# Layer 0 of a four-layer gated transformer kernel: value products placed behind the next four heads' scores, the output bias added early, two norms cut into smaller steps

## The chip, the cores and the metric

The kernel runs on one core of a Trainium2 chip. The metric is the time of one execution on the device in microseconds (us), and the number to predict is the median of several executions of the changed kernel. The engines that the text names are PE (TensorE: matrix products and, with an identity matrix, transposes), DVE (VectorE), ACT (ScalarE), POOL (GpSimd) and SP (SyncE, which issues most transfers here). PE writes its results to a small memory, PSUM; DVE or ACT has to copy them out before the PSUM buffer can be used again. Each engine works through its own list of instructions in order. Between engines there are only semaphores: an instruction that waits holds up everything behind it on its engine.

## The reference

The program is a stack of four layers on x of 8 batches x 256 tokens x 512 channels, each layer being `x = x + tanh(g) * attention(layernorm(x))` and then `x = x + tanh(g') * ffn(layernorm(x))`. Only layer 0 is touched by the change. Cut to what matters:

```python
# layer 0, cross attention, 16 heads of 32 channels, quantised linear maps
q = w8a8_linear(layernorm(x), wq, bq)            # per token: s = max|x|/127, round(x/s)
k, v = ctx @ wk.T + bk, ctx @ wv.T + bv
o = softmax(q @ k.T / sqrt(32) + mask) @ v
x = x + tanh(g0) * w8a8_linear(o, wo, bo)        # quantised per token again, then + bo
# layer 0, feed-forward: one of 8 experts of rank 64 per token
lg = layernorm(x) @ Wg.T;  e = argmax(softmax(lg))
x = x + tanh(g1) * 4 * prob[e] * ((layernorm(x) @ A[e].T) @ Bw[e].T)
```

Layers 1 to 3 (linear attention with 64 experts, channel attention with a dense feed-forward, a recurrence with 8 experts) follow and are the same before and after.

## The kernel before

The 2048 tokens lie in 16 tiles `xt[i]` of 128 tokens x 512 channels, which stay in the core's memory. Layer 0 goes through four blocks of 512 tokens (`blk`), each of two batches (`bb` 0 and 1; batch number `b = 2*blk + bb`). `attend0` handles one batch. Its 16 heads are taken in four groups `j` of four. A group is: the scores `s` of its four heads (L521, eight products that use 32 rows of the array each, four side by side), and then for each head `r` two maxima over the scores (L541, DVE), two exponentials with their sums (L546, ACT), four transposes of the probabilities (`pt`, L553, PE), and one copy of them to `pT` (L105 on DVE or L107 on ACT, in turn). After the four heads come the group's value products `oT` (L562), their copy `oTs`, two transposes `o` (L573), and the multiplication by the reciprocal sums into `ao` (L575, L576).

Beside the attention of block `blk` other work is threaded in. After each head, `step()` (L477) advances the projection of the batch before by one step, and a generator `others(blk)` by a rate of steps per head (`due`, L480: 0.65 in block 0, 1.1 in blocks 1 and 2, 0.9 in block 3). `others` mixes (L458) two steps of `tokens()` with one step of `context()`:

- `context()` makes keys (4 steps, L308) and values (4 steps, L313) of the next block, or in the last block keys of layer 1 (`keys1`). One such step is four products of 128x128 by 128x512.
- `tokens()` first waits, with empty steps, until the projection of the batch before is done (`while proj`), then runs the expert layer of block `blk - 1` (`experts`, L344: one step for the norm of four token tiles, two for their transposes `tr_f`, one for the router's logits `lgk`, `lgp`, and twelve for the products `h` and `y` with the experts' weights), and then the queries of block `blk + 1` (`queries`, L321: one step for the norm of four tiles, four in which a tile is quantised and transposed, four for the products `q0ps`).

`project()` (L583) quantises `ao` (two steps), transposes it (`trq_o`, two steps), and multiplies by `wo` (two steps). Each of the last two ends with three operations: DVE scales the product into `y` (L597), POOL adds the bias `gbo` to `y` (L598), POOL adds `y` to `xt[i]` (L599). A norm is: `bn_stats` and `bn_aggr` of each tile on DVE (L160, L163), one addition (`ve`, L167), a power on POOL (`rstd`, L169), and the subtraction and scaling of each tile on DVE (`xn`, L179).

A planner at compile time puts the instructions on the engines' lists. It takes them in the order in which the program makes them, except that an instruction whose inputs and buffers the planner's own clock shows ready can go ahead of one that is not ready. The scores have a raised priority (L517), and the first four of a group may start only when the last maximum of the group before is done (L530). Buffers bound how far this goes: six `pT` tiles, two PSUM banks `tr` (transposes and `oT`), two `ac` (`o` and the threaded work), four `mm` (scores), six tiles `b8` (keys, values, queries, turned tokens), four `xn`.

Of the kernel before, what the change touches and what calls it, by code (L numbers as in the profile page):

```python
# [11 lines left out]
F32 = mybir.dt.float32  # L12
# [3 lines left out]
ALU = mybir.AluOpType  # L16
# [4 lines left out]
P = 128  # L21
C = 512
KC = C // P
B, S = 8, 256
# [25 lines left out]
def flamingo_kernel(ctx: ExitStack, tc: tile.TileContext, a):  # L50
# [210 lines left out]
    def front():  # L261
# [57 lines left out]
                yield  # L319

        def queries(blk, bank):  # L321
            xns = norm(blk, "a0")
            yield
            qxT = qxp.tile([P, KC, BLK], BF16, tag="qx", name=f"qxT{blk}")
            sx_ps = bank(f"sx_ps{blk}")
            for i in range(TB):
                q, s = quantise(xns[i], f"x{blk}_{i}")
                transpose4_q(qxT[:, :, ts(i, P)], q, f"x{blk}_{i}")
                spread(sx_ps[:, ts(i, P)], s, f"x{blk}_{i}")
                yield  # L330
            sx = t2.tile([P, BLK], F32, tag="t2", name=f"sx{blk}")
            nc.scalar.copy(sx, sx_ps)
            Q[blk] = b8.tile([P, KC, BLK], F32, tag="b8", name=f"Q0_{blk}")
            for j in range(KC):
                ps = bank(f"q0ps{blk}_{j}")
                matmul_k(ps, [qT["wq0"][:, k, ts(j, P)] for k in range(KC)], [qxT[:, k, :] for k in range(KC)])
                nc.vector.scalar_tensor_tensor(Q[blk][:, j, :], ps, swq[:, j : j + 1], sx, ALU.mult, ALU.mult)
                nc.gpsimd.tensor_scalar(Q[blk][:, j, :], Q[blk][:, j, :], bq[:, j : j + 1], None, ALU.add)
                yield
# [1 line left out]

        AB = []

        def experts(blk, bank, halves=1):  # L344
            A, Bw = AB
            xnT = b8.tile([P, KC, BLK], F32, tag="b8", name=f"xnT_f0{blk}")
            n = TB // halves
            for half in range(halves):
                xns = norm_of(range(blk * TB + half * n, blk * TB + half * n + n), f"f0{blk}_{half}_")
                yield  # L350
                for i in range(n):
                    transpose4(xnT[:, :, ts(half * n + i, P)], xns[i], f"f0{blk}_{half * n + i}")
                    if i % 2:
                        yield
            lg = logits(xnT, wg, f"f0{blk}")
            yield
            best = best_of_8(lg, 1, f"f0{blk}")

            _, rz = softmax_8(lg, f"f0{blk}")
            nc.vector.tensor_scalar(rz, rz, tg[:, 4:5], 4.0, ALU.mult, ALU.mult)  # L360
            h, hT = {}, {}

            def first(i):
                ps = bank(f"h0_{blk}_{i}")
# [12 lines left out]

            def second(i):
                ps = bank(f"y0_{blk}_{i}")
                matmul_k(ps, [hT[i][:, k, :] for k in range(KC)], [Bw[:, k, :] for k in range(KC)])  # L380
                add_scaled(blk * TB + i, ps, rz[:, i : i + 1])


            first(0)
            yield
            for i in range(TB):
                if i + 1 < TB:
                    first(i + 1)
                    yield
                turned(i)  # L390
                yield
                if i:
                    second(i - 1)
                    yield
            second(TB - 1)
            yield
# [9 lines left out]
        def others(blk):  # L406
# [15 lines left out]

            def tokens():
                if blk:
                    while proj:
                        yield
                    yield from experts(blk - 1, actile)
                if blk + 1 < NB:
                    yield from queries(blk + 1, actile)
                else:  # L430
                    for _ in range(2):
                        yield next(last_experts)

            def context():
                if blk + 1 < NB:
                    yield from keys(blk + 1, actile)
                    yield from values(blk + 1, actile)
                else:
                    yield from keys1(0, actile)
                    yield next(last_keys)  # L440

            yield from mix(tokens(), context(), 2)

# [8 lines left out]
                nc.scalar.activation(K1[:, j, :], ps, AF.Identity, bias=first1["bk"][:, j : j + 1])  # L452
                yield

        last_experts = experts(NB - 1, mmtile, 2)
        last_keys = keys1(1, mmtile)

        def mix(one, two, n):  # L458
# [10 lines left out]
                    yield  # L469

        aos = []
        proj, last_max = [], []
        for blk in range(NB):
            gen = others(blk)
            due = [0.0]
# [1 line left out]
            def step():  # L477
                if proj and next(proj[0], 0) is not None:
                    proj.pop()
                due[0] += (0.65, *(NB - 2) * (1.1,), 0.9)[blk]  # L480
                while due[0] >= 1.0:
                    due[0] -= 1.0
                    next(gen, None)
# [1 line left out]
            if blk == 0:  # L485
                next(gen)
            for bb in range(BLK // S):
                one = attend0(blk, bb, Q[blk], K[blk], V[blk], qT["wo0"], gswo, gbo, aos[0], last_max, step)
                proj.append(one)
            for _ in gen:  # L490
                pass

        for n, _ in enumerate(proj[0]):
            if n == 1:
                next(last_keys)
        next(last_experts)
        for _ in last_keys:
            pass
        for _ in last_experts:
            pass  # L500

    def attend0(blk, bb, Q, K, V, woT, gswo, gbo, aos, last_max, step):

# [7 lines left out]
        s16 = sm.tile([P, 2, NH], F32, tag="s16", name=f"s16_{b}")  # L511
        rs = sm.tile([P, 2, NH], F32, tag="rs16", name=f"rs_{b}")
        ao = aos[:, b % 2]
        for j in range(KC):
            nm = f"{b}_{j}"
            ps = [mm.tile([P, 2, S], F32, tag="mm", name=f"s_{nm}_{r}") for r in range(4)]
# [20 lines left out]
            for r in range(4):  # L537
# [15 lines left out]
                        nc.tensor.transpose(pt_ps[:, lt, nt, :], pr[:, nt, ts(lt, P)], ident)  # L553
                pT.append(ptp.tile([P, 2, S], F32, tag="pT", name=f"pT_{nm}_{r}"))
                evac(pT[r], pt_ps.rearrange("p l n q -> p l (n q)"))
                step()
            last_max.append(one)
            oT_ps = tr.tile([P, S], F32, tag="tr", name=f"oT_{nm}")
            for lt in range(2):
                for r in range(4):  # L560
                    rows = slice(HD * r, HD * r + HD)
                    nc.tensor.matmul(  # L562
                        oT_ps[rows, :],
                        V[:, bb * 2 + lt, ts(4 * j + r, HD)],
                        pT[r][:, lt, :],
                        start=(lt == 0),
                        stop=(lt == 1),
                    )
            oT = sm.tile([P, S], F32, tag="oT", name=f"oTs_{nm}", bufs=2)
            evac(oT, oT_ps)  # L570
            o = ac.tile([P, 2, 4, HD], F32, tag="ac", name=f"o_{nm}")
            for nt in range(2):
                nc.tensor.transpose(o[:, nt].rearrange("p h d -> p (h d)"), oT[:, ts(nt, P)], ident)  # L573
            heads = slice(4 * j, 4 * j + 4)
            nc.vector.reciprocal(rs[:, :, heads], s16[:, :, heads])  # L575
            nc.vector.tensor_tensor(  # L576
                ao[:, :, ts(j, P)].rearrange("p n (h d) -> p n h d", d=HD),
                o,
                rs[:, :, heads].unsqueeze(3).to_broadcast([P, 2, 4, HD]),
                ALU.mult,  # L580
            )

        def project():  # L583
            qs, qoT = [], []
# [7 lines left out]
            for nt in range(2):  # L592
# [2 lines left out]
                i = b * 2 + nt  # L595
                y = t2.tile([P, C], F32, tag="t2", name=f"y_{b}_{nt}")
                nc.vector.scalar_tensor_tensor(y, ps, qs[nt][1], gswo, ALU.mult, ALU.mult)  # L597
                nc.gpsimd.tensor_tensor(out=y, in0=y, in1=gbo, op=ALU.add)  # L598
                nc.gpsimd.tensor_tensor(out=xt[i], in0=xt[i], in1=y, op=ALU.add)  # L599
                yield  # L600

        return project()
# [43 lines left out]

    def logits(xnT, w, name):

        part = ac.tile([P, BLK], F32, tag="ac", name=f"lgk_{name}")
        last = None  # L650
        for k in range(KC):
# [3 lines left out]
            last = one  # L655
        turned = t2.tile([P, BLK], F32, tag="t2", name=f"lgt_{name}")
        evac(turned, part)
        ps = ac.tile([P, TB, 8], F32, tag="ac", name=f"lgp_{name}")
        for i in range(TB):
            nc.tensor.matmul(ps[:, i, :], turned[:, ts(i, P)], pick8, start=True, stop=True)  # L660
        lg = sm.tile([P, TB, 8], F32, tag="lg8", name=f"lg_{name}", bufs=2)
        nc.vector.tensor_copy(lg, ps)
        return lg
# [1780 lines left out]
```

## Time and profile before

| what | before |
|---|---|
| median of 6 runs | 2644.27 us (2637.74 to 2646.49) |
| the profiled execution, its own time | 2644.52 us |
| span from its first to its last instruction | 2642.7 us, mean granted PE clock 0.971 |
| PE, DVE, ACT, POOL busy over the span | 94%, 48%, 24%, 34% |
| layer 0's attention | first scores at 53.6 us, last value products from 508.9 us |
| layer 0's last expert product | issued from 552.4 us, layer 1's first products from 559.3 us |

The page of a profile gives busy time by engine for the whole span and for 40 slices of 66 us each; layer 0 fills the first eight. Another view gives the same for any stretch of time, with the clock that PE was granted there as a share of full speed. A third lists who waited for whom; "PE s L521 <- DVE n L541: 3.4, 2, 1.7" says that PE sat idle before `s` of line 521 for 3.4 us in all, in 2 places, 1.7 us the longest, and that DVE's `n` of line 541 ended the wait. The timeline gives instructions in order of time, each with its start, its duration, engine, line, operation and tiles, and in brackets the idle time of its engine just before it. PE's ends are modelled, so a PE that is busy all the time is not necessarily at its peak.

### The profile page before, as it was taken

To read this page: it belongs to the slowest core of one execution; us is meant where nothing else is said; L and a number is where in the kernel's file an instruction comes from. 1 tells how busy PE (TensorE), PEld (TensorE's weight loads), DVE (VectorE), ACT (ScalarE), POOL (GpSimd) and SP (SyncE) were. 2 spreads that over 40 slices of the span, in tenths; PEclk is the share of its full clock that TensorE was granted. 3 is DMA by queue.
4 is the path that set the end of the run, shared out by engine and by line. 5 is a ranking of instruction groups with operands and counts; after the bars stand their busy time and mean duration, and the time that the engine had idled before them with its cause. 6 is when DMAs were issued, how large, how long until landed. Compare 5 with 4: busy or idle time off the path is not lost. (4 is left out here: it accounts for less than half of the span.)

```text
span 2642.7 us, 29842 instructions
## 1 busy us (share of the span) xinstructions
PE 2475.2 (94%) x10389; PEld 1272.5 (48%) x10404; DVE 1277.9 (48%) x3518; ACT 643.6 (24%) x1451; POOL 901.6 (34%) x843
## 2 busy tenths in 40 slices
PE   7889898899999979999999899899999999999997
PEld 3445454456655535545555344444444444455553
DVE  6656565536656442222222650767677766211111
ACT  1534344311111112222222111222222222111110
POOL 1110211111344344656665110231534252444542
PEclk9999999998999989999999999999999999999999
DMA  5000010112112127999997741112022212788984
GB/s 219 5 21 25 17 41 5 33 37 80 50 33 65 44 80 219 243 263 267 286 256 169 236 168 68 40 72 104 32 96 91 89 37 52 236 292 291 322 280 89
DMA packets 102180, 333.75 MB, mean 126 GB/s; under 512 B 23288, under 2 KB 25721, under 8 KB 93827
## 3 DMA queue, kind: packets, MB, share of 16 engines
q0 software_dynamic: 48256, 148.74, 21.1%
q1 hardware_dynamic: 50354, 178.73, 19.3%
q10 hardware_dynamic: 3408, 4.25, 0.5%
q8 instruction: 87, 1.43, 0.2%
q14 instruction: 75, 0.61, 0.1%
HBM read 283.35 MB, written 66.88 MB: 133 GB/s over the span
## 5 line engine op out<-in xcount | busy, mean ns | idle before, releaser
L1335 PE MATMUL gu<-w,eb 128*128 128x352 f32 (+1 forms) x1064 | 240.7, 463 | 3.4 <-DMA w<-in_w 3.4
L216 PE MATMUL h2p<-xnT_f,p 128*128 128x512 f32 x512 | 226.9, 598 | 5.7 <-issue 4.4
L216 PE MATMUL o2f<-p,h 128*128 128x512 f32 x512 | 226.0, 595 | 3.3 <-ACT h L1628 3.2
L1370 POOL DMA_INDIRECT acc<-eb,who x94 | 147.4, 1568 | 134.5 <-DVE eb L105 107.5
L1012 POOL DMA_INDIRECT table<-pay,rowi x128 | 125.3, 979 | 138.8 <-PE v L216 44.5
L1335 PEld LDWEIGHTS gu<-w,eb 128*128 128x128 f32 (+1 forms) x1064 | 129.8, 159 | 72.3 <-issue 19.5
L546 ACT ACTIVATE pr<-pr,n 128x256 f32<-128x256 f32 x256 | 127.9, 501 | 149.5 <-DVE n L541 144.6
L216 PEld LDWEIGHTS h2p<-xnT_f,p 128*128 128x128 f32 x512 | 97.0, 192 | 123.4 <-issue 118.5
L216 PEld LDWEIGHTS o2f<-p,h 128*128 128x128 f32 x512 | 95.7, 190 | 122.6 <-issue 114.7
L1387 POOL DMA_INDIRECT xg<-xnd,who x94 | 99.4, 1057 | 64.0 <-PE ehp L1355 20.2
L227 DVE SCALAR_TENSOR_TENSOR x<-o2f,tg,x 128x512 f32<-128x512 f32 x64 | 46.9, 741 | 125.2 <-PE o2f L216 123.7
L598 POOL TENSOR_TENSOR y<-y,gbo 128x512 f32<-128x512 f32 x16 | 20.3, 1271 | 245.4 <-DVE y L597 237.9
L1984 PE MATMUL g_r<-w3gu,xgT 128*128 128x352 f32 (+1 forms) x336 | 102.5, 467 | 0.7 <-ACT xgT L107 0.7
L169 POOL TENSOR_TENSOR rstd_a<-ve_a,mhalf 128x4 f32<-128x4 f32 x15 | 15.7, 1043 | 253.9 <-DVE ve_a L167 252.7
L541 DVE CUSTOM_DVE_ANT_0 pr<-s,mask 128x256 f32<-128x256 f32 x256 | 96.8, 417 | 11.1 <-PE s L521 6.7
L1984 PE MATMUL u_r<-w3gu,xgT 128*128 128x352 f32 (+1 forms) x336 | 100.0, 459 | 0.0
L1993 DVE SCALAR_TENSOR_TENSOR h_r<-a_r,share,u_r 128x352 f32<-128x352 f32 x33 | 19.2, 580 | 160.7 <-PE u_r L1984 152.1
L2010 PE MATMUL d_r<-w3d,hT_r 128*128 128x512 f32 (+3 forms) x252 | 96.1, 596 | 0.0
L1628 ACT ACTIVATE h<-h2p,b 128x512 f32<-128x512 f32 x64 | 43.4, 686 | 213.5 <-PE h2p L216 213.3
L553 PE MATMUL pt<-ident,pr 128*128 128x128 f32 x512 | 85.3, 286 | 9.8 <-ACT pr L546 5.8
L1406 PE MATMUL ed<-w,eb 128*128 128x512 f32 (+1 forms) x266 | 91.5, 601 | 1.6 <-DVE eb L1356 1.6
L553 PEld LDWEIGHTS pt<-ident,pr 128*128 128x128 f32 x512 | 59.6, 143 | 64.8 <-issue 28.4
(586 smaller groups left out, 4729.5 us busy)
## 6 DMA issues: line engine op xcount, KB each, us to landing
w<-in_w SPq DMA_DIRECT2D x64, 960.0 KB
p<-in_p SPq DMA_DIRECT2D x64, 512.0 KB
acc<-xnd SPq DMA_DIRECT2D x48, 256.0 KB
more<-acc SPq DMA_DIRECT2D x48, 256.0 KB
xnd<-xn_f SPq DMA_DIRECT2D x32, 256.0 KB
wd<-in_wd SPq DMA_DIRECT2D x64, 96.0 KB
ctxTa<-in_ctxT SPq DMA_DIRECT2D x4, 1024.0 KB
x<-in_x SPq DMA_DIRECT2D x16, 256.0 KB
```

The costliest lines, as they stand in the source:

```text
L216: one = nc.tensor.matmul(ps, lhsT[k], rhs[k], start=(k == 0), stop=(k == n - 1))
L227: return nc.vector.scalar_tensor_tensor(xt[i], ps, scale, xt[i], ALU.mult, ALU.add)
L541: one = nc.vector.tensor_tensor_reduce(pr[:, nt, :], ps[r][:, nt, :], mask[:, nt, :], -1.0, -LOW, ALU.add, ALU.min, n16[:, nt, h : h + 1],)
L546: nc.scalar.activation(pr[:, nt, :], pr[:, nt, :], AF.Exp, bias=n16[:, nt, h : h + 1], scale=-1.0, accum_out=s16[:, nt, h : h + 1],)
L553: nc.tensor.transpose(pt_ps[:, lt, nt, :], pr[:, nt, ts(lt, P)], ident)
L1012: one = nc.gpsimd.indirect_dma_start(out=table[:, :], out_offset=bass.IndirectOffsetOnAxis(ap=rows, axis=0), in_=choice, in_offset=None, b ...
L1335: one = nc.tensor.matmul(gu[part, 0 : 2 * I1], xT[:, k, part], e.gu[:, k, :], start=(k == 0), stop=(k == KC - 1))
L1370: one = nc.gpsimd.indirect_dma_start(out=acc[0][:, :], out_offset=bass.IndirectOffsetOnAxis(ap=index[:stop, col : col + 1], axis=0), in_=s ...
L1387: nc.gpsimd.indirect_dma_start(out=xg, out_offset=None, in_=xnd[:, :], in_offset=bass.IndirectOffsetOnAxis(ap=who[:, col : col + 1], axis= ...
L1406: one = nc.tensor.matmul(ps[n][part, :], t.hT[rows, k, part], wd, start=(k == 0), stop=(k == 1))
L1984: one = nc.tensor.matmul(ps[part, 0:I3], xTt[:, k, part], wgu[k][:, g, :], start=(k == 0), stop=(k == KC - 1))
L2010: one = nc.tensor.matmul(ps[part, :], hT[:cn, n, part], wd[n][:cn], start=(n == 0), stop=(n == 2))
```

## The change

All of it is in layer 0.

1. The part of `attend0` that follows the four heads (value products, copy, transposes, division) becomes a function `outputs(j, pT)`. It is put in a list `late` and called in the first head of the next group, behind that head's `pT` copy and ahead of its `step()`. For the last group of a batch that is the first head of the next batch, or a call after the loop.
2. The bias `gbo` is added to `xt[i]` on POOL at the start of each batch's `attend0`. `project()` loses its bias addition, and its addition to `xt[i]` moves from POOL to DVE in the second batch of a block (`bb` 1).
3. `experts` norms two tiles at a time in every block (the argument `halves` goes), one step for each tile's statistics and one for the two scalings. Only the second two tiles, those of the batch still being projected, wait for `proj`. The logits take two more steps (`logits_steps`). `queries` gets one step per tile for its statistics.
4. The rates per head rise from 1.1 to 1.45 and from 0.9 to 1.1. In the last block `tokens()` takes one step of `last_keys` and four of `last_experts` in place of two; `context()` loses its step of `last_keys`. After the loop three steps of `last_experts` follow the projection in place of one.

```diff
         def queries(blk, bank):
-            xns = norm(blk, "a0")
+            for stats in stats_of(range(blk * TB, blk * TB + TB), f"a0{blk}"):
+                yield
+            xns = normed(stats, f"a0{blk}")
             yield
...
-        def experts(blk, bank, halves=1):
+        def experts(blk, bank):
             A, Bw = AB
             xnT = b8.tile([P, KC, BLK], F32, tag="b8", name=f"xnT_f0{blk}")
-            n = TB // halves
-            for half in range(halves):
-                xns = norm_of(range(blk * TB + half * n, blk * TB + half * n + n), f"f0{blk}_{half}_")
-                yield
-                for i in range(n):
-                    transpose4(xnT[:, :, ts(half * n + i, P)], xns[i], f"f0{blk}_{half * n + i}")
-                    if i % 2:
+            for half in range(2):
+                if half:
+                    while proj:
                         yield
-            lg = logits(xnT, wg, f"f0{blk}")
+                name = f"f0{blk}_{half}_"
+                for stats in stats_of(range(blk * TB + half * 2, blk * TB + half * 2 + 2), name):
+                    yield
+                xns = normed(stats, name)
+                yield
+                for i in range(2):
+                    transpose4(xnT[:, :, ts(half * 2 + i, P)], xns[i], f"f0{blk}_{half * 2 + i}")
+                yield
+            lg = yield from logits_steps(xnT, wg, f"f0{blk}")
             yield
...
             def tokens():
                 if blk:
-                    while proj:
-                        yield
                     yield from experts(blk - 1, actile)
                 if blk + 1 < NB:
                     yield from queries(blk + 1, actile)
                 else:
-                    for _ in range(2):
+                    yield next(last_keys)
+                    for _ in range(4):
                         yield next(last_experts)
...
                     yield from keys1(0, actile)
-                    yield next(last_keys)
...
-                due[0] += (0.65, *(NB - 2) * (1.1,), 0.9)[blk]
+                due[0] += (0.65, *(NB - 2) * (1.45,), 1.1)[blk]
...
+        late.pop()()
         for n, _ in enumerate(proj[0]):
             if n == 1:
                 next(last_keys)
-        next(last_experts)
+        proj.pop()
+        for _ in range(3):
+            next(last_experts)
...
         ao = aos[:, b % 2]
+        for i in range(b * 2, b * 2 + 2):
+            nc.gpsimd.tensor_tensor(out=xt[i], in0=xt[i], in1=gbo, op=ALU.add)
+        def outputs(j, pT):
+            oT_ps = tr.tile([P, S], F32, tag="tr", name=f"oT_{nm}")
...
                 evac(pT[r], pt_ps.rearrange("p l n q -> p l (n q)"))
+                if late:
+                    late.pop()()
                 step()
             last_max.append(one)
-            oT_ps = tr.tile([P, S], F32, tag="tr", name=f"oT_{nm}")
...
+            late.append(lambda j=j, pT=pT: outputs(j, pT))
...
                 nc.vector.scalar_tensor_tensor(y, ps, qs[nt][1], gswo, ALU.mult, ALU.mult)
-                nc.gpsimd.tensor_tensor(out=y, in0=y, in1=gbo, op=ALU.add)
-                nc.gpsimd.tensor_tensor(out=xt[i], in0=xt[i], in1=y, op=ALU.add)
+                (nc.vector if bb else nc.gpsimd).tensor_tensor(out=xt[i], in0=xt[i], in1=y, op=ALU.add)
                 yield
...
+    def logits_steps(xnT, w, name):
...
         evac(turned, part)
+        yield
         ps = ac.tile([P, TB, 8], F32, tag="ac", name=f"lgp_{name}")
         for i in range(TB):
             nc.tensor.matmul(ps[:, i, :], turned[:, ts(i, P)], pick8, start=True, stop=True)
+        yield
         lg = sm.tile([P, TB, 8], F32, tag="lg8", name=f"lg_{name}", bufs=2)
```

More of the change, by code (lines that the diff above doesn't have):

```diff
@@ L453, in keys1 @@
                 yield
-        last_experts = experts(NB - 1, mmtile, 2)
+        last_experts = experts(NB - 1, mmtile)
         last_keys = keys1(1, mmtile)
@@ L471, in front @@
         aos = []
-        proj, last_max = [], []
+        proj, last_max, late = [], [], []
         for blk in range(NB):
@@ L487, in front @@
             for bb in range(BLK // S):
-                one = attend0(blk, bb, Q[blk], K[blk], V[blk], qT["wo0"], gswo, gbo, aos[0], last_max, step)
+                one = attend0(blk, bb, Q[blk], K[blk], V[blk], qT["wo0"], gswo, gbo, aos[0], last_max, late, step)
                 proj.append(one)
@@ L500, in front, with attend0 @@
             pass
-    def attend0(blk, bb, Q, K, V, woT, gswo, gbo, aos, last_max, step):
+    def attend0(blk, bb, Q, K, V, woT, gswo, gbo, aos, last_max, late, step):
         b = blk * (BLK // S) + bb
@@ L513, in attend0 @@
         ao = aos[:, b % 2]
+        for i in range(b * 2, b * 2 + 2):
+            nc.gpsimd.tensor_tensor(out=xt[i], in0=xt[i], in1=gbo, op=ALU.add)
+        def outputs(j, pT):
+            nm = f"{b}_{j}"
+            oT_ps = tr.tile([P, S], F32, tag="tr", name=f"oT_{nm}")
+            for lt in range(2):
+                for r in range(4):
+                    rows = slice(HD * r, HD * r + HD)
+                    nc.tensor.matmul(
+                        oT_ps[rows, :],
+                        V[:, bb * 2 + lt, ts(4 * j + r, HD)],
+                        pT[r][:, lt, :],
+                        start=(lt == 0),
+                        stop=(lt == 1),
+                    )
+            oT = sm.tile([P, S], F32, tag="oT", name=f"oTs_{nm}", bufs=2)
+            evac(oT, oT_ps)
+            o = ac.tile([P, 2, 4, HD], F32, tag="ac", name=f"o_{nm}")
+            for nt in range(2):
+                nc.tensor.transpose(o[:, nt].rearrange("p h d -> p (h d)"), oT[:, ts(nt, P)], ident)
+            heads = slice(4 * j, 4 * j + 4)
+            nc.vector.reciprocal(rs[:, :, heads], s16[:, :, heads])
+            nc.vector.tensor_tensor(
+                ao[:, :, ts(j, P)].rearrange("p n (h d) -> p n h d", d=HD),
+                o,
+                rs[:, :, heads].unsqueeze(3).to_broadcast([P, 2, 4, HD]),
+                ALU.mult,
+            )
         for j in range(KC):
@@ L555, in attend0 @@
                 evac(pT[r], pt_ps.rearrange("p l n q -> p l (n q)"))
+                if late:
+                    late.pop()()
                 step()
             last_max.append(one)
-            oT_ps = tr.tile([P, S], F32, tag="tr", name=f"oT_{nm}")
[L559 to L581, printed above, removed]
+            late.append(lambda j=j, pT=pT: outputs(j, pT))
         def project():
@@ L647, in logits @@
     def logits(xnT, w, name):
+        steps = logits_steps(xnT, w, name)
+        while True:
+            try:
+                next(steps)
+            except StopIteration as end:
+                return end.value
+    def logits_steps(xnT, w, name):
         part = ac.tile([P, BLK], F32, tag="ac", name=f"lgk_{name}")
```

## Prediction

> **What bounds the kernel now.** I read the page first, for the engine that fills the span and for the clock.
>
> ```profile
> PE 2475.2 (94%) x10389; PEld 1272.5 (48%) x10404; DVE 1277.9 (48%) x3518; ACT 643.6 (24%) x1451; POOL 901.6 (34%) x843
> PE   7889898899999979999999899899999999999997
> PEclk9999999998999989999999999999999999999999
> ```
>
> PE is the bound, and layer 0 (slices one to eight) has more 8s in PE's row than the rest. Then layer 0 by stretches; the columns are length, busy time of PE, weight loads, DVE, ACT and POOL (with counts), and PE's granted clock.
>
> ```profile
> 155.00:188.00 33.00, 25.61 (x163) 14.24 (x162) 21.89 (x71) 14.40 (x45) 7.09 (x6) 0.95 0.01 1
> 188.00:267.00 79.00, 76.08 (x424) 40.00 (x424) 51.27 (x174) 33.74 (x106) 6.29 (x5) 1.00 0.06 21
> 279.00:313.00 34.00, 25.32 (x166) 14.15 (x165) 21.06 (x72) 14.56 (x46) 7.08 (x6) 0.95 0.01 1
> 313.00:392.00 79.00, 75.42 (x422) 39.81 (x423) 52.25 (x174) 32.89 (x103) 6.21 (x5) 1.00 0.13 47
> 404.00:429.00 25.00, 17.95 (x120) 9.90 (x120) 14.74 (x52) 12.45 (x43) 6.08 (x5) 0.87 0.00 1
> 520.00:532.00 12.00, 8.39 (x25) 3.50 (x24) 3.61 (x8) 1.78 (x3) 3.82 (x4) 0.72 0.18 74
> ```
>
> The middle of a block (188 to 267, 313 to 392) is full: PE is busy 96% of it. The loss sits near the start of blocks 1, 2 and 3 (7.4, 8.7 and 7.1 us of idle PE) and in the tail (3.6), and there the clock is low too. The waits of PE between 53 and 552 us say on what; of these lines the last number is the longest wait.
>
> ```profile
> PE oT L562 <- DVE pT L105: 7.4, 7, 4.7
> PE tr_f L194 <- DVE xn_f__0_4455 L179: 3.6, 1, 3.6
> PE s L521 <- DVE ve_f__2594 L167: 2.4, 1, 2.4
> PE s L521 <- DVE ve_f__1538 L167: 2.3, 1, 2.3
> ```
>
> Four single gaps, one in each of those stretches, together 4.75 + 3.61 + 2.40 + 2.33 = 13.1 us (starts 425.7, 525.9, 293.5, 169.5). The timeline shows what stands before one of them.
>
> ```profile
> 286.58 1.27 POOL L598 TENSOR_TENSOR y<-y,gbo 128x512 f32<-128x512 f32 x1 [10.50 <-DVE y L597]
> 287.93 1.27 POOL L599 TENSOR_TENSOR x<-x,y 128x512 f32<-128x512 f32 x1
> 289.17 1.27 POOL L598 TENSOR_TENSOR y<-y,gbo 128x512 f32<-128x512 f32 x1
> 289.24 0.69 DVE L160 BATCH_NORM_STATS2 bn_f__2_2588<-x 128x6 f32<-128x512 f32 x1 [0.77 <-POOL x L599]
> 290.51 1.26 POOL L599 TENSOR_TENSOR x<-x,y 128x512 f32<-128x512 f32 x1
> 291.81 0.69 DVE L160 BATCH_NORM_STATS2 bn_f__3_2591<-x 128x6 f32<-128x512 f32 x1 [1.88 <-POOL x L599]
> 293.46 1.15 PE L521 MATMUL s<-K,Q 32*128 32x256 f32 x16 [2.40 <-DVE ve_f__2594 L167]
> ```
>
> POOL's four additions take 5.2 us in a row. DVE's statistics wait for them, and behind these on DVE's list stand the maxima of the running heads (292.50, 292.91), for which ACT and then PE wait.
>
> **The change part by part.** The sum is made against the profiled execution, 2644.52 us (span 2642.7, 1.8 around it), which lies 0.25 above the median.
>
> *Bias and addition.* In the second batch of a block the way from `y` to the statistics is now one DVE addition. Nearest row: `V<-v0ps,bv`, also 128x512, 0.69 us. From the end of the second `y` to the start of the last statistics took 287.78 to 291.81, 163.91 to 167.94, 415.46 to 419.50 (4.0 each) and 518.7 to 523.2 (4.5); with one addition it is 0.7, so 3.3 and 3.8 us go. A gap can close by no more: 2.33 + 2.40 + 3.3 + 2.8 (in the last, 0.83 us of DVE waiting for the power on POOL stays) = 10.8 us. Late next are gaps of the same stretches, 2.71 us at 298.6 (`tr_f` after `pT`) and 1.59 at 174.7, in which four tiles are scaled in a row ahead of the maxima. I take three quarters, **-8.1**; ends 0 and -10.8. The eight additions cost DVE 8 x 0.69 = 5.5 us, hidden where DVE is busy 64% (21.9 of 33); uncovered they cost 5.5, which offsets a part of this term. POOL has 16 bias additions of 1.27 us as before, at the start of a batch; there its list also holds the queries' bias (1.59 each), for which scores wait. At block 2's start the last of these ended at 276.07 and the scores of the next group began at 279.47, so 2 x 1.27 fits; if not, 2.5 us in each of three blocks.
>
> *Clock.* Lost at the low clock in the four stretches: 0.05 x 33 + 0.05 x 34 + 0.13 x 25 + 0.28 x 12 = 10.0 us. I take **-4**: half of what follows the four gaps (8.3; the rest is a drop at 409, elsewhere). Ends 0 and -10. On this the Trainium skill (TensorE: Matmul & The Clock Gate, "HAM oscillation") speaks against me: it has the clock halved by gaps over about 3.4 us, so shortening 2.33 and 2.40 would earn no clock, and this term would be some 1.7 us smaller. The trace has low clock in both stretches, 0.95, with no gap there over 2.71.
>
> *Steps.* I laid the steps of blocks 1 and 2 out in the program's order, a head at a time. PE: a group of heads 4.2 us (16 transposes at 0.108 start to start, `s` 1.07, `oT` 1.00, `o` 0.4), a key, value or expert product 8 x 0.429 = 3.43, four transposes 0.43, a query product 4 x 0.216 = 0.86. DVE: a group 6.2 (eight maxima at 0.417 + 0.084, two copies at 0.69, 0.8 for the rest). Before: 35 steps in 32 heads, four of them empty; two query products are left over and run bare at the end. After: 46 steps, two empty, none left. In the first eight heads PE work goes from 18.3 to 21.7 us, into a stretch that idles 7.4 to 8.7: up to -3.4 in each of two blocks. In the last eight heads now stand only the queries: PE 13.6 against DVE 29.8 us, where before two expert products were among them, 18.8 against 30.5 with 1.7 left over. PE can idle 16.2 there instead of 11.7 (+1.7 bare is in the block either way): up to +4.5 in each. The planner softens both, since it lets ready work go ahead: queries' statistics of block 3 (`bn_a`) ran at 293.3, far ahead of their step. I take **+2.2**, the sum of both ends; ends -6.8 and +9. Block 0 gets four more steps at an unchanged rate (21 in 20.8), one value step is left over, not needed before the second batch: 0. The extra `ve` and power in three blocks, 0.17 and 1.04 us, have a step between them and the scaling: 0; if DVE waits, 1.2 each, as at 421.8.
>
> *Value products.* Their waits for `pT` (7.4 + 1.9) and those of `o` for `oTs` (5.5) can shrink, but the 4.75 is counted above, so 10.1 is left, and the planner already has the scores ahead: those of the group at 250.4 precede the value products of the group before, at 259.1. I take **-2**; ends -5.1 (all of the `oT` part bar 4.75) and, at seven changes of batch, DVE waiting for `o` before quantising, now in the same step: up to 2.3 us each on DVE, of which PE feels what the quarter of maxima behind it is late, +4. Buffers: four `pT` stay until one head into the next group, which has two more; the third head's copy would wait for the value products, put two heads (2 x 3.9 us) earlier: 0, uncovered one wait of 1.07. The values tile is held one head longer, while keys and queries of its block are free already: 0.
>
> *Moves.* `last_keys` and `last_experts` change places by a few steps, with the same products: 0. No moved step issues a transfer, so SP's and ACT's lists keep their order; the mask's load stays first in a batch. Layer 1's `Wv` is issued at 514.2 and used at 559.3, 45 us of cover.
>
> Sum: -8.1 - 4 + 2.2 - 2 = -11.9, so 2632.6 for the profiled execution and 2632 for the median.
>
> **Rivals.**
>
> 1. *Queries alone become the bound* (the other side). Place: last eight heads of blocks 1 and 2. Price +9 if the planner keeps the program's order. For it: DVE 29.8 against PE 13.6. Against: `bn_a` at 293.3. It decides when the other terms give less than 9 us; without them the time is 2653.5.
> 2. *The change hardly changes the order*: scores already run ahead of value products, statistics ahead of their steps. Then only the POOL part counts in the tail, 2.8, and the rest cancels: 2642.
> 3. *The starts of the blocks fill up*: all ends on the good side, -10.8 - 10 - 6.8 - 5.1 = -32.7, 2612. For it: PE fills 96% where it has threaded work. Against: the starts keep maxima, quantising and norms on one DVE.
>
> **How the numbers follow.** Forecast 0.50 (its own range 2622 to 2639), rival 1 0.22, rival 2 0.15, rival 3 0.13 (2612 to 2622). The range runs from 2612 (all gains) to 2655, rival 1 with half of the three extra power waits (1.8); beyond it I leave some 0.17. A change within 0.2% (5.3 us) is about what a measurement cannot tell from none. Faster by more: forecast 0.47, rival 3 0.13, some of rival 2 0.04, together 0.64. Within: the rest of rival 2, 0.11, and bits of the forecast and rival 1, 0.03 and 0.02: 0.16. Slower: 0.20.
>
> **What the profile after would show.** If the first part is right, no `bn_f` in an odd batch waits for POOL, and the gaps of 2 to 5 us before `s`, `oT` and `tr_f` at the block starts are gone, with clock 1.00 there. If the steps are right, scores of a block start closer together early on and PE stays over 90% busy in its last eight heads; if rival 1 is, those heads show PE under 60% and DVE over 90%. The rest of the program, from the first `v<-Wv` to the end, should keep its length of about 2083 us. I am wrong if DVE's list in the new order puts norms or quantising ahead of the maxima elsewhere, or if layers 1 to 3 change length, which no term here holds.

## The result and the profile after

| | before | after |
|---|---|---|
| median | 2644.18 us (43 runs, 2636.86 to 2650.97) | 2653.58 us (20 runs, 2645.82 to 2660.36) |
| ratio to before | | 1.0034, 95% interval 1.0026 to 1.0043 |
| span of the profiled execution | 2642.7 us | 2657.3 us |
| first `s` | 53.6 us | 56.8 us |
| end of the last `oT` of layer 0 | 510.0 us | 535.6 us |
| first `v<-Wv` of layer 1 | 559.3 us | 578.7 us |
| from there to the end | 2083.4 us | 2078.6 us |

The change made the kernel 0.34% slower, some 9 us, where 2632 us and a gain were forecast. The loss lies in layer 0: 3.2 us before the first scores and 22.4 us more until the last value products, of which the tail gives 6.2 back. That leaves 19.4 us, more than the 9 by which the medians differ, since a profile shows one execution: the rest of the program, the same code in both, was 4.8 us shorter in this one, and 5.0 us longer (2088.4 us) in a second profiled execution of the changed kernel. Two rows of the page after:

```profile
PE 2486.4 (94%) x10391; PEld 1273.9 (48%) x10404; DVE 1289.5 (49%) x3529; ACT 644.2 (24%) x1451; POOL 896.2 (34%) x838
...
PEclk8989999999999899999999999999999999999999
```

PE's busy sum is 11.2 us larger with two instructions more, and PEclk has an 8 in slices one and three, where it had 9s. Layer 0 by stretches (length; busy time of PE, weight loads, DVE, ACT, POOL with counts; then PE's clock):

```profile
142.00:192.00 50.00, 42.75 (x235) 21.67 (x236) 29.43 (x95) 19.16 (x60) 3.41 (x3) 0.93 0.06 22
192.00:287.00 95.00, 87.17 (x459) 45.06 (x459) 57.54 (x190) 34.97 (x109) 11.23 (x9) 0.95 0.05 18
287.00:325.00 38.00, 30.98 (x203) 16.84 (x208) 26.03 (x89) 19.03 (x60) 5.46 (x5) 0.96 0.00 1
325.00:414.00 89.00, 81.21 (x450) 42.47 (x446) 59.88 (x189) 33.03 (x104) 11.23 (x10) 1.00 0.12 42
414.00:447.00 33.00, 27.08 (x188) 14.22 (x189) 24.40 (x84) 18.03 (x58) 5.27 (x4) 0.95 0.00 1
447.00:516.00 69.00, 63.19 (x328) 32.57 (x328) 36.52 (x124) 25.46 (x80) 3.26 (x3) 0.92 0.01 5
```

The stretches that began the blocks (142, 287, 414) still idle, by 7.3, 7.0 and 5.9 us. What is new is the middle of blocks 1 and 2: 7.8 us of idle PE in 192 to 287 and 7.8 in 325 to 414, where 2.9 and 3.6 were idle in the 79 us that were shown of each before, and a clock of 0.92 in the last block's threaded part. The waits of PE name it, before (53 to 552 us) and after (53 to 572 us):

```profile
PE pt L553 <- ACT pr L546: 5.8, 12, 1.2
```

```profile
PE pt L590 <- ACT pr L583: 21.4, 19, 2.8
PE pt L590 <- ACT pT L107: 7.0, 4, 3.2
```

`pt` waiting for ACT's exponential was 5.8 us in 12 places before. It is 21.4 us in 19. The four single gaps behind POOL's additions, which the forecast set out to remove (13.1 us), are gone but for 0.9 us in the tail, and none of the statistics `bn_f` of an odd batch waits for POOL any more. PE's idle time in gaps over 0.1 us, from the first scores to the first `Wv` product, is 54.6 us against 53.1: it has moved, not shrunk. The timeline in one of the new gaps (start, duration, engine, line, operation; in brackets the idle time before and what ended it):

```profile
252.28 0.69 DVE L373 TENSOR_TENSOR h0s<-h,best_f 128x512 f32<-128x512 f32 x1 [3.06 <-PE h L216]
252.89 0.41 DVE L578 CUSTOM_DVE_ANT_0 pr<-s,mask 128x256 f32<-128x256 f32 x1
...
253.34 0.51 ACT L583 ACTIVATE pr<-pr,n 128x256 f32<-128x256 f32 x1 [4.19 <-DVE n L578]
...
254.00 0.44 PE L590 MATMUL pt<-ident,pr 128*128 128x128 f32 x2 [1.76 <-ACT pr L583]
...
254.37 0.62 PE L530 MATMUL oT<-pT,V 128*32 128x256 f32 x2
...
255.29 1.06 PE L530 MATMUL oT<-pT,V 128*32 128x256 f32 x14
```

PE ends the expert product `h`. DVE multiplies it, takes the first maxima of the new group, ACT takes the exponential, and until that is there PE has 1.76 us of nothing. The value products of the group before, all of whose inputs are there, come behind the first two transposes of the first head's `pt` on PE's list. The scores of this group had been done since 246.9; it is not for them that PE waits.

The same group (the sixth of block 1) before, from its timeline:

```profile
231.25 1.07 PE L562 MATMUL oT<-pT,V 128*32 128x256 f32 x16
231.35 0.69 DVE L367 TENSOR_TENSOR h0s<-h,best_f 128x512 f32<-128x512 f32 x1 [2.74 <-PE h L216]
231.96 0.41 DVE L541 CUSTOM_DVE_ANT_0 pr<-s,mask 128x256 f32<-128x256 f32 x1
...
232.65 0.51 ACT L546 ACTIVATE pr<-pr,n 128x256 f32<-128x256 f32 x1
...
232.81 0.44 PE L573 MATMUL o<-ident,oTs 128*128 128x128 f32 x2 [0.49 <-ACT oTs L107]
...
233.08 0.38 PE L216 MATMUL wo<-qT,qoT 128*128 128x512 bf16 x1
...
233.51 0.38 PE L553 MATMUL pt<-ident,pr 128*128 128x128 f32 x2
```

DVE waits for `h` and takes the same maximum, ACT the same exponential; but PE has the value products, `o` and a product of `wo` in the meantime, idles 0.49 us before `o`, and `pt` follows without a wait that counts. The value products were the work that covered the chain from `h` to the exponential.

### The profile page after: what moved, and what is told of

The parts are those of the page before. It is cut to its first block, busy times and chain, and to the rows that moved or that the text cites. A ratio compares the mean times of both kernels' runs of the same rounds, so it can differ in the third digit from the quotient of the medians.

```text
span 2657.3 us, 29856 instructions
## 1 busy us (share of the span) xinstructions
PE 2486.4 (94%) x10391; PEld 1273.9 (48%) x10404; DVE 1289.5 (49%) x3529; ACT 644.2 (24%) x1451; POOL 896.2 (34%) x838
## 5 line engine op out<-in xcount | busy, mean ns | idle before, releaser
L590 PE MATMUL pt<-ident,pr 128*128 128x128 f32 x512 | 89.3, 290 | 31.0 <-ACT pr L583 21.4
L614 POOL TENSOR_TENSOR x<-x,y 128x512 f32<-128x512 f32 x8 | 10.2, 1276 | 241.2 <-DVE y L613 241.1
```

## The experiments

Five theories were set against each other. V: the place of the value products, behind the first head's `pt`, is the loss. W: it is their lateness as such, wherever they stand. S: the smaller steps and the higher rates of steps are. B: the early bias additions are. P, added after the first set: POOL's additions beside DVE's scaling delay the starts of the blocks. The sets of runs were made on different chips. In the second, the kernel before takes 2604.37 us (11 runs), so across sets only ratios to it compare.

### First set: each part alone, and the change without its first part (before: 2644.64 us)

`late_only`: before, with the value products deferred and nothing else.

```diff
                 evac(pT[r], pt_ps.rearrange("p l n q -> p l (n q)"))
+                if late:
+                    late.pop()()
                 step()
             last_max.append(one)
-            oT_ps = tr.tile([P, S], F32, tag="tr", name=f"oT_{nm}")
...
+            late.append(lambda j=j, pT=pT: outputs(j, pT))
```

> Before, with part 1 alone: the value products of a group are called behind the next group's first head. Theory V (the value products no longer stand between a group's scores and its first transposes, so PE waits there for the exponentials): slower than before by 5 to 14 us, PE's wait of the transposes pt for the exponentials pr between 53 and 575 us goes from 5.8 us to over 15, and PE's time at half clock in layer 0 from 20 us to over 30. Theory S (the steps and rates are the loss): within 5 us of before. Theory B (the bias additions on POOL are the loss): within 5 us of before.

`no_late`: after, with the value products back at the end of their own group.

```diff
-                if late:
-                    late.pop()()
                 step()
             last_max.append(one)
-            late.append(lambda j=j, pT=pT: outputs(j, pT))
+            outputs(j, pT)
```

> The changed kernel with part 1 undone: value products straight after their four heads, all else as changed. Theory V: at or under the time of before, 2630 to 2644 us, with the wait of pt for pr back under 10 us. Theory S: 2649 to 2660 us, as changed. Theory B: 2649 to 2660 us.

`bias_only`: before, with the bias added at the start of a batch and DVE's addition in odd batches.

```diff
+        for i in range(b * 2, b * 2 + 2):
+            nc.gpsimd.tensor_tensor(out=xt[i], in0=xt[i], in1=gbo, op=ALU.add)
...
-                nc.gpsimd.tensor_tensor(out=y, in0=y, in1=gbo, op=ALU.add)
-                nc.gpsimd.tensor_tensor(out=xt[i], in0=xt[i], in1=y, op=ALU.add)
+                (nc.vector if bb else nc.gpsimd).tensor_tensor(out=xt[i], in0=xt[i], in1=y, op=ALU.add)
```

> Before, with part 2 alone: bias added on POOL at the start of each batch, addition to x on DVE in every second batch. In the changed profile the scaling xn_a beside these additions took 1.01 us on average, up to 1.50, against 0.55 us without them, and layer 0's first products came 2.3 us later. Theory B: slower than before by 5 to 12 us. Theories V and S: from 6 us faster (the four gaps behind POOL gone) to 2 us slower (the late start).

`steps_only`: before, with the two norms cut into steps and the new rates.

```diff
-            xns = norm(blk, "a0")
+            for stats in stats_of(range(blk * TB, blk * TB + TB), f"a0{blk}"):
+                yield
+            xns = normed(stats, f"a0{blk}")
...
-                due[0] += (0.65, *(NB - 2) * (1.1,), 0.9)[blk]
+                due[0] += (0.65, *(NB - 2) * (1.45,), 1.1)[blk]
```

> Before, with parts 3 and 4 alone: norms in smaller steps, logits in three, higher rates, last_experts earlier. Theory S (queries stand alone in the last eight heads of blocks 1 and 2, where PE starves): slower than before by 5 to 12 us, PE under 75% busy in those heads. Theories V and B: from 8 us faster to 3 us slower.

| kernel | median | ratio to before (95%) |
|---|---|---|
| `late_only` | 2671.08 us | 1.0108 (1.0086 to 1.0130) |
| `no_late` | 2632.65 us | 0.9962 (0.9947 to 0.9977) |
| `bias_only` | 2644.73 us | 1.0009 (0.9996 to 1.0023) |
| `steps_only` | 2639.99 us | 0.9985 (0.9972 to 0.9997) |

The deferral alone costs 26.4 us, more than the whole change loses and well over the 5 to 14 us that V expected; without it the change gains 12.0 us. S falls: the steps are worth a small gain. B falls as a cause of the loss: the bias part is worth nothing either way. The waits of PE in `late_only` (first scores to first `Wv` product) carry the verdict:

```profile
PE pt L581 <- ACT pr L574: 24.2, 18, 4.4
```

The parts do not add up: 26.4 + 0.1 - 4.7 is 21.8, and the change loses 9. The larger part of this lies between the bias and the steps, which give 0.1 and -4.7 us alone and -12.0 together (`no_late`). The deferral costs 26.4 us alone and some 21 on top of the two (24 in the third set). Why the two are worth more together than apart, no run here shows.

### Second set: where the value products stand (before: 2604.37 us)

`ahead`: after, with the deferred products moved by a few lines, from behind the first head's transposes to ahead of them.

```diff
+                if late:
+                    late.pop()()
                 pt_ps = tr.tile([P, 2, 2, P], F32, tag="tr", name=f"pt_{nm}_{r}")
...
                 evac(pT[r], pt_ps.rearrange("p l n q -> p l (n q)"))
-                if late:
-                    late.pop()()
                 step()
```

> The changed kernel with one move: the call of the value products in the next group's first head stands ahead of that head's transposes pt and no longer behind them and their copy. Theory V (PE's list has lost the work between the scores and the first transposes): PE's wait of pt for the exponentials pr is back under 10 us, time 2628 to 2644 us, near the kernel without part 1 (2632.65). Theory W (lateness as such: pT tiles held longer, ao and so the projection late): 2649 to 2660 us, as changed (2653.58).

Measured: 2593.16 us, 0.9958 (0.9944 to 0.9972). The loss is gone, as V expected: PE's waits for the exponential before `pt` fall from 21.4 us to 5.4, and waits of `oT` for `pT` come back, 14.9 us. It is no better than having them at the end of their own group (0.9962 in the first set). It does not separate V from W, for the planner lets the value products go almost as early as in `no_late`: from the end of a group's last `pT` copy to its first value product there are 0.46 us on average, against 0.36 in `no_late` and 1.70 in the change. What speaks against W is in the traces of the third set: the projection, which lateness would hold up, makes PE wait 3.9 us before `trq_o` and `wo` in the change and 3.5 without the deferral. That is an argument, not a test.

`fill`: after, with eight needless transposes of the identity ahead of each first head's `pt`.

```diff
+                if r == 0:
+                    for n in range(8):
+                        nc.tensor.transpose(pt_ps[:, n // 4, n // 2 % 2, :], ident, ident)
                 for nt in range(2):
```

> The changed kernel with eight extra transposes of the identity matrix ahead of the transposes of each group's first head, 32 x 8 x 0.109 = 28 us of needless work on PE, which stand where PE waits for the exponentials. Theory C (half of the loss is PE's clock, halved after stretches with such waits): the time lost to the low clock between the first scores and layer 1's first values, 22.2 us in the changed profile, falls under 15 us, and the kernel is slower than the changed one by less than 14 us. Theory I (the clock has nothing to do with these waits): clock loss stays at 19 us or more and the kernel is slower by 14 us or more.

Measured: 2626.16 us, 1.0087 (1.0068 to 1.0106). Against the change's 1.0034 that is 14 us for 28 us of added work, from ratios of two chips. Side by side with the change it is in the third set.

`bias_later`: `no_late`, with the two bias additions of a batch held until the last maximum of the batch's first group.

```diff
-        for i in range(b * 2, b * 2 + 2):
-            nc.gpsimd.tensor_tensor(out=xt[i], in0=xt[i], in1=gbo, op=ALU.add)
...
         for j in range(KC):
+            if j == 1:
+                for i in range(b * 2, b * 2 + 2):
+                    add = nc.gpsimd.tensor_tensor(out=xt[i], in0=xt[i], in1=gbo, op=ALU.add)
+                    tc.add_manual_dep(add.ins, last_max[-1].ins.name, ...)
```

> The changed kernel without part 1 and with the bias additions on POOL held until the last maximum of the batch's first four heads, so that none runs beside the scaling xn_a. Theory P (POOL's additions slow DVE's scaling: 16 scalings from 1.0 us back to 0.55, first scores 2 to 3 us earlier): 2624 to 2631 us, 2 to 8 us under the kernel without part 1 (2632.65). Theory Q (the slower scalings are hidden, apart from the start): 2630 to 2635 us.

Measured: 2589.13 us, 0.9946 (0.9928 to 0.9964).

`ahead_later`: `ahead` with the same edit to the bias additions.

> Both: value products in the next group's first head ahead of its transposes, and the bias additions held back as in the run before. If both theories V and P hold: 2622 to 2632 us, the fastest of all. If the value products so placed are worse than straight after their heads: above that run by 3 us or more.

Measured: 2591.23 us, 0.9953 (0.9935 to 0.9970). Both ratios lie a little below those of their parents (0.9962, 0.9958), within the intervals, so P was left undecided by this set.

### Third set: four kernels side by side (before: 2644.31 us, 18 runs)

> The changed kernel unchanged, so that it stands on one chip with the next three. If the ratio of a kernel to the kernel before belongs to the kernel and not to the chip, it is 1.0034 again (1.0026 to 1.0043). If the chip decides how much the clock gives away, it is lower on a chip whose times are shorter, and less than 22 us go to the half clock in layer 0.

> The changed kernel with eight needless transposes of the identity ahead of each first head's own transposes, 28 us of added TensorE work, once more beside the changed kernel itself. If TensorE idles there for want of work and nothing else, the added work lies in the idle time: within 7 us of the changed kernel. If half of it fits, 14 us above it (the ratio of the first look, 1.0087 against 1.0034). If the stretch is full, 28 us above it.

> The changed kernel with the value products back at the end of their own group. Theory V (the place of the value products is the whole loss): 0.9962 again, 19 us under the changed kernel on the same chip. If that gain was the chip's, it shrinks to under 10 us here.

> The kernel without late value products, with the two bias additions of a batch held until the last maximum of the batch's first group. Theory P (POOL's additions beside DVE's scaling delay the starts of the blocks): 0.9946 again, 3 to 5 us under the kernel without late value products. The rival (the slower scaling is off the path, and holding the additions only moves them): within 2 us of it.

| kernel | median | ratio to before (95%) |
|---|---|---|
| the change again | 2650.52 us | 1.0023 (1.0011 to 1.0035) |
| `fill` again | 2659.12 us | 1.0054 (1.0035 to 1.0072) |
| `no_late` again | 2626.43 us | 0.9932 (0.9913 to 0.9950) |
| `bias_later` again | 2625.25 us | 0.9932 (0.9910 to 0.9954) |

V a third time: 24.1 us between the change and the same without its deferral, where 19 had been expected. The change's own ratio lies below its first, 1.0034, with intervals that overlap. Where the 24.1 us lie is seen in two tables of the same program stretches, cut at the same instructions (the first line is the whole, from the first `s` to the first `Wv` product; then block 1 from its third group to its end, block 2's first two groups, block 2 from its third group, and block 3 from its third group to its last `oT`). The change:

```profile
55.50:573.80 518.30, 461.49 (x2569) 240.91 (x2581) 317.61 (x1057) 210.43 (x653) 51.71 (x61) 0.97 0.08 25
189.50:283.20 93.70, 85.75 (x471) 44.65 (x473) 58.91 (x196) 36.46 (x114) 11.32 (x10) 0.98 0.06 18
283.20:316.90 33.70, 26.87 (x175) 14.57 (x176) 23.22 (x79) 15.88 (x49) 5.34 (x4) 1.00 0.00 1
316.90:410.30 93.40, 85.33 (x471) 44.91 (x473) 61.87 (x199) 36.06 (x115) 11.14 (x10) 0.98 0.12 40
439.60:530.70 91.10, 84.44 (x460) 44.05 (x461) 47.14 (x162) 38.54 (x120) 3.26 (x3) 0.94 0.01 4
```

And `no_late`:

```profile
55.40:545.20 489.80, 447.21 (x2569) 237.21 (x2581) 316.35 (x1057) 209.97 (x653) 51.21 (x60) 0.99 0.08 27
181.50:270.70 89.20, 84.78 (x475) 45.67 (x477) 60.73 (x196) 35.48 (x114) 11.18 (x10) 0.98 0.06 19
270.70:303.30 32.60, 27.03 (x176) 14.36 (x177) 23.13 (x79) 15.78 (x49) 5.29 (x4) 1.00 0.00 1
303.30:390.90 87.60, 83.06 (x471) 44.44 (x473) 59.73 (x199) 37.07 (x115) 11.14 (x10) 1.00 0.12 43
421.20:502.10 80.90, 78.72 (x454) 42.15 (x455) 45.99 (x157) 36.84 (x116) 3.26 (x3) 0.98 0.01 4
```

The whole is 28.5 us shorter, with the same 2569 PE instructions. (That is more than the medians differ by: this execution of the change, 2663.96 us, is the slowest of its twelve.) 14.2 us of it are idle PE (56.8 against 42.6), and 14.3 us are busy time, which goes with a clock of 0.97 against 0.99. The three threaded stretches are shorter by 4.5, 5.8 and 10.2 us, the beginning of block 2 only by 1.1, and the tail, not shown, by nothing (43.1 us in both); of the other two that are left out, the one up to block 1's third group is 7.9 shorter and the beginning of block 3 is 1.0 longer. The waits of PE in `no_late`:

```profile
PE oT L529 <- DVE pT L105: 8.0, 8, 2.9
PE oT L529 <- ACT pT L107: 7.2, 6, 3.2
PE pt L589 <- ACT pr L582: 3.4, 7, 0.7
```

and its timeline at the group that was shown of the change:

```profile
237.17 1.07 PE L529 MATMUL oT<-pT,V 128*32 128x256 f32 x16
...
237.89 0.41 DVE L577 CUSTOM_DVE_ANT_0 pr<-s,mask 128x256 f32<-128x256 f32 x1
...
239.44 0.38 PE L589 MATMUL pt<-ident,pr 128*128 128x128 f32 x2
```

This is the order of before again. The 15.2 us that `oT` waits for `pT` here are the price of this place. The deferral removes 12.6 of them, and pays 18.1 more for `pr` (21.5 against 3.4) and 5.1 more for `pT` before `pt` (6.9 against 1.8), together 10.6 of the 14.2 us; the rest is spread over smaller waits. That is shown as far as idle time goes, and the other pair of profiles agrees (the change's first has 56.3 us idle in this stretch, `no_late`'s first 41.9).

The clock is another matter. In the three profiles with the deferral behind `pt` and no needless work it is 0.96, 0.97 and 0.96 in this stretch, in the others between 0.97 and 0.99, so the two overlap. `bias_later` again, with the value products at the end of their groups too, has the 0.97 of the change:

```profile
53.30:548.80 495.50, 455.47 (x2570) 242.03 (x2582) 315.77 (x1050) 210.13 (x653) 59.56 (x67) 0.97 0.08 26
```

At this equal clock the stretch is 22.8 us shorter than in the change, 16.8 of it idle time. So most of the loss is there without any difference in clock; what the 6.0 us of busy time are stays open, and that the deferral's gaps lower the clock is not shown.

`fill` lies 8.6 us over the change, between the first two of its expectations, with intervals that just touch. Its profile over the same stretch, and its wait for the exponential:

```profile
55.80:585.50 529.70, 488.52 (x2826) 270.95 (x2838) 317.83 (x1057) 210.08 (x653) 51.64 (x61) 0.97 0.08 25
```

```profile
PE pt L593 <- ACT pr L583: 5.4, 11, 1.3
```

PE is busy 27.0 us longer than in the change, and the stretch is 11.4 longer, so 15.6 us of needless work ran in time that was idle. The wait for `pr` fell by 16.1. So the gaps are places where PE had nothing on its list to run, not the mark of a slower exponential. That half of the loss is the clock, lowered by these waits (C in the expectations of the first `fill`), is not borne out: with the waits filled the clock is 0.97, as in the change.

P is not shown as a gain: with the bias additions held, the first scores start at 53.3 instead of 55.4 us, but the time is that of `no_late` within 1.2 us, and the interval, some 6 us on either side, allows no more to be said. `no_late` beats the kernel before by 10 to 18 us by its ratios, and the change by 19 to 24; holding the additions adds nothing that was measured.

## Why the prediction was wrong

- **Value products** (-2, ends -5.1 and +4) is the step that failed. Measured: +26.4 us alone, +24.1 within the change. The step said that `pT` waits can shrink and that "the planner already has the scores ahead". Both are true: the waits of `oT` for `pT` fell from 9.3 us to 1.8. But it looked only at what the value products wait for, and not at what waits while they run. The row that it quoted, scores at 250.4 and value products at 259.1, was from the last group of a block, where the first maximum (251.8) is long done and a deferral costs nothing: in the same group of the change `pt` waits for nothing. The sixth group, some 20 us earlier on the same timeline and shown above, has the answer: the value products run from 231.25 beside DVE's multiplication and first maximum, for which PE would otherwise wait. In the change such a wait of 1.4 to 3.2 us stands before the first `pt` in 11 of the 32 groups, 22.8 us in all; in nine ACT's exponential ends it, in two ACT's copy `pT` behind the exponentials. In six of the 11 DVE has `h0s` ahead of the first maximum, in four the experts' norm, in one the router's logits. In `no_late` no first `pt` waits as long as 1 us, though the norms stand ahead of the maxima there too; norms in that place were the prediction's own sign of being wrong. The upper end, +4, counted a late quantising on DVE; the cover that was taken off PE had no row in the sum. For what was added the working named the work that hides it; for what was moved away it did not ask what it had been hiding.
- **Bias and addition** (-8.1, ends 0 and -10.8): right in the tail, not at the starts of the blocks. The tail gained what was forecast for it. The end of the last `oT` to the first `Wv` product, in `bias_only`:

```profile
518.90:562.80 43.90, 42.89 (x139) 20.07 (x141) 19.27 (x46) 5.11 (x9) 3.55 (x22) 1.00 0.32 103
```

and before:

```profile
510.00:559.30 49.30, 45.63 (x139) 21.29 (x141) 18.30 (x44) 5.11 (x9) 8.56 (x26) 0.93 0.30 92
```

  It is 5.4 us shorter: 2.7 of idle PE (3.7 to 1.0), where 2.8 had been taken, and 2.7 of busy time, with the clock at 1.00 instead of 0.93. At the starts of the blocks the three gaps only shrank, from 2.33, 2.40 and 4.75 us to 1.58, 1.70 and 3.64, and the two that were "late next" grew, from 1.59 and 2.71 to 2.76 and 3.63. PE in `bias_only` at block 1:

```profile
175.87 1.15 PE L523 MATMUL s<-K,Q 32*128 32x256 f32 x16 [1.58 <-DVE ve_f__1540 L167]
...
181.05 1.11 PE L194 MATMUL tr_f<-ident,xn_f__1_1546 128*128 128x128 f32 x4 [2.76 <-DVE pT L105]
```

  The first scores came 2.7 us later. Together the part measured 2.4 us on the slow side by its ratio, between -1 and +6. The "three quarters" were a choice without a row; the end at 0 was the truth.
- **Steps** (+2.2, ends -6.8 and +9): `steps_only` measured -4.0 us by its ratio (-0.8 to -7.4), so the sign was wrong and the time lies between the middle and the good end.
- **Clock** (-4, ends 0 and -10): the clock of the stretch fell to 0.96 and 0.97, from 0.98. In the change the four gaps went and others came in their place. The Trainium skill (TensorE: Matmul & The Clock Gate, "HAM oscillation") gives the rule that PE should have no idle gaps over about 3.4 us. As a warning against the gain it was weighed rightly, but the clock was halved here with no gap over 3.2 us, as shown below.
- *Queries alone become the bound*: its time, 2653.5, is the measured one, but by chance. Its place is the last two groups of blocks 1 and 2, which after the change read:

```profile
265.60:287.10 21.50, 18.81 (x146) 11.19 (x146) 18.57 (x64) 13.00 (x44) 2.30 (x3) 1.00 0.04 13
392.70:413.90 21.20, 18.24 (x146) 11.08 (x146) 18.68 (x63) 13.94 (x45) 2.29 (x3) 1.00 0.04 14
```

  DVE is busy 86% and 88%, PE 87% and 86%, and the stretches last 21.5 and 21.2 us, where the same groups took 27.4 and 27.7 with expert products among them. The working had put 13.6 us of PE and 29.8 of DVE there; the planner had moved part of the queries' work ahead (statistics `bn_a` ran as early as 185 us), and PE had 18.8 and 18.2, DVE 18.6 and 18.7. Neither "PE under 60%" nor "DVE over 90%" is there, nor the "over 90%" of PE that the steps were to give, and `steps_only`, which holds these heads, is no slower than before.
- *The rest of the program keeps its length*: 2078.6 us against 2083.4; right within what executions differ by. The sum without the value products, -9.9 with the clock, is near what `no_late` measured by its ratio, -10.0 in the first set and -18.0 in the third. That is in part luck: alone the bias part measured +2.4 and the steps -4.0, each with its clock, where -8.1 and +2.2 had been taken and -4 for the clock.

## What to carry to other kernels

Before moving work to where its own inputs are surely ready, look at what it covers where it stands: work with ready inputs between a product and the first use of a two-engine chain (here maximum on DVE, exponential on ACT) can be worth as much as that chain is long, in each group where nothing else covers it (here 11 of 32). If it has to be deferred, it belongs into that hole, ahead of the first instruction that waits for the chain, not behind it. And a sum of an engine's idle time tells less than its list of waits: here the sum stayed at 53 to 55 us while every large entry in it changed.

## What the runs showed of the hardware that was not expected

DVE's scaling of a tile (`xn_a`, 128x512, one input and its output both in SBUF) is slowed by additions on POOL that run at the same time. The tile's row after the change, minimum, median and maximum in ns:

```profile
L179 DVE TENSOR_SCALAR xn_a<-x,mv_a,rstd_a x20: 539/546/1498, 25.5 to 585.7; 128x512 f32<-128x512 f32 x20
```

Its maximum had been 548. The planner puts each bias addition right behind the scaling that last reads its tile, so the four run side by side at the start of the program:

```profile
25.51 3.81 DVE L179 TENSOR_SCALAR xn_a<-x,mv_a,rstd_a 128x512 f32<-128x512 f32 x4 [0.54 <-POOL rstd_a L169]
...
26.13 5.53 POOL L522 TENSOR_TENSOR x<-x,gbo 128x512 f32<-128x512 f32 x4 [0.66 <-DVE xn_a L179]
...
31.89 0.55 PE L258 MATMUL sx_ps<-diag_x,ones 128*128 128x128 f32 x1 [4.29 <-DVE diag_x L257]
```

Four scalings take 3.81 us instead of 1.92, POOL's four additions 5.53 instead of 4 x 1.27, and the first `sx_ps` starts at 31.9 us instead of 29.6. With the additions held until the first group's maxima (`bias_later` again) the row has 537, 541 and 548 ns, and before the change 537, 544 and 548. But another scaling of DVE, `qb_x`, then meets an addition once and takes 1.50 us instead of 0.48, so holding them moved a part of this.

DVE's maxima and its copies out of PSUM kept their time beside POOL (in the change 419 ns on average alone and 420 beside one of its 128x512 operations; 689 and 683). The Trainium skill (SBUF — State Buffer, "SBUF: two separate sides") names a port pair that DVE and GpSimd lock against each other for whole instructions. The longest scaling here, 1.50 us, is shorter than a scaling and a whole addition after each other (0.55 + 1.27), so the rows agree with a wait for the rest of an addition that had begun; that the port is the reason, no run here shows. The prediction's sum held nothing for these additions, since POOL had room for them; it had asked whose list they stand on, and not what runs beside them.

PE's clock was halved without a long gap. Two stretches of the change, one with the 3.17 us gap at 190.5 and one with the 1.98 us gap at 230.7:

```profile
190.00:196.00 6.00, 5.51 (x41) 2.80 (x42) 4.51 (x16) 3.42 (x13) 2.35 (x2) 0.72 0.01 3
229.00:238.00 9.00, 6.69 (x30) 3.20 (x31) 5.37 (x19) 2.15 (x7) 0.00 (x0) 0.81 0.00 0
```

No gap of PE between 57 and 572 us is longer than 3.2 us in this execution. In the other profiled execution of the same kernel the 1.98 us gap, at 228.1, cost no clock:

```profile
226.40:235.40 9.00, 6.72 (x35) 3.10 (x36) 6.03 (x20) 2.28 (x7) 0.00 (x0) 1.00 0.00 0
```

So a gap of this size can go with a halved clock but need not, and two executions of one program differ by several us in it. What decides between them stays open here.
